# An LSTM recurrence on one core: partial sums placed ahead of an addition that waits, two more buffers, a shorter warm-up

## The chip, the cores and the metric

The kernel runs on one core of a Trainium2 chip. The metric is device time in microseconds of one execution, as the median of several runs. Below, TensorE is PE in the profile, VectorE is DVE, ScalarE is ACT, GpSimd is POOL, and SP is the queue of SyncE, which issues nearly all DMAs.

## The reference

An LSTM over 512 time steps with a batch of 32, 512 inputs and 512 hidden units, all in float32, whose hidden states are added to the input.

```python
xW = jnp.einsum('ntd,dg->ntg', x, Wx) + b          # 32 x 512 x 2048
def step(carry, xw_t):
    prev_h, prev_c = carry
    a = xw_t + prev_h @ Wh
    i, f, o = (jax.nn.sigmoid(a[:, k * Hd:(k + 1) * Hd]) for k in range(3))
    g = jnp.tanh(a[:, 3 * Hd:])
    next_c = f * prev_c + i * g
    next_h = o * jnp.tanh(next_c)
    return ((next_h, next_c), next_h)
out = x + hs                                        # hs: next_h of all steps
```

## The kernel before

Two kinds of work share the core. The first is the chain of time steps. Step k is `h_part(k)`, 32 products of the transposed h with Wh (line L667, 64 TensorE instructions), then `cell(k)`: three activations on ScalarE (L690 to L692), the cell's products and sum on VectorE (L693 to L695), a tanh (L696), h (L697) and its transposition (L702), which the next `h_part` waits for. GpSimd adds h to x for the output (L706) and, in `add_bias` (L648), the bias to the x product that `load_xw` (L645) has fetched for a later step; ScalarE copies that into PSUM as the seed of the gates (L654, L658).

The second is x times Wx, which fills TensorE behind each `h_part`. The first rows of eight time steps are done directly or in units (the head, until window `START` = 21, step 17). After that, rounds of 24 steps make three rows each: twenty products of sums of blocks of x with sums of blocks of Wx, each product again by seven smaller ones (line L412). A step k belongs to window v = k + 4, and its place in the round is (k - 17) mod 24, so that step 0 of a round opens it. Five of six windows start a new product (`begin`), and its seven parts are spread over windows v to v + 4 by `products`.

On the other engines a window's work is given out in a fixed order, and each engine works its own list in order:

- `evacuate(v)`: additions that are overdue; then `finish` of the second half of the product that began five windows ago and of the first half of that of four windows ago: half additions out of PSUM on VectorE (L559) or copies on ScalarE (L547); then ScalarE's copies of a newer product's accumulators (L440, L444), the addition L447 on VectorE, and for the product of three windows ago ScalarE's copies L451 and L452 into the PSUM tile `pp`, and VectorE's addition L453 into the same tile behind them.
- `run_due(v, room)`: from the list `due`, sorted by window, whatever is due, and then what fits in a room counted in columns (128 for a sum plus `FIXED` = 160, 512 for a node, 1024 for a whole addition). In it are sums of four blocks of x (L375 to L378, the x sums, which are a product's left factors), nodes (L347, sums of whole blocks of x), whole additions of products (L575), and in the head the sums of Wx's blocks (L246, L250).
- then `products(v)` for TensorE, `fetch(v)` for SyncE (factors of later products, rows of x), and `cell(k)`.

A half or whole addition takes its target from the list `free`, first in, first out: four tiles `slot`, and from `START` on four tiles that held blocks of Wx and their sums. A finished sum is stored to DRAM by four DMAs (`store`, L469) and its tile goes back to the list.

The head's x sums (`inner_sums`, L279 to L282) have four tiles of their own in the pool `spool`, one for each pair (row, half). Before the first products 24 matmuls on zeros are issued (L787).

Of the kernel before, what the change touches and what calls it, by code (L numbers as in the profile page):

```python
# [9 lines left out]
F32 = mybir.dt.float32  # L10
# [4 lines left out]
P = 128  # L15
B = 32
T = 512
NJ = 4
# [4 lines left out]
C = 256  # L23
# [21 lines left out]
NODES = 8  # L45
FIXED = 160
ROOM = 3400
HEAD_ROOM = 5000
SLACK = [1, 1, 3]
AHEAD = 3  # L50
# [54 lines left out]
def windows_of(k):  # L105

    return [k + 4]


START = windows_of(HEAD - LEAD)[0]  # L110
# [14 lines left out]
def kernel(  # L125
# [13 lines left out]
    spool = ctx.enter_context(tc.tile_pool(name="spool", bufs=4))  # L139
# [66 lines left out]
    def t_sums(i):  # L206
        w, t = raw[i], tt_[i]
        return [
            lambda: nc.vector.tensor_sub(t[:, 0:2], w[:, 1::2], w[:, 0:2]),
            lambda: nc.vector.tensor_sub(t[:, 2], w[:, 3], t[:, 0]),  # L210
            lambda: nc.vector.tensor_sub(t[:, 3], w[:, 2], t[:, 2]),
        ]

    def raw_factor(i, s):
        return raw[i][:, {1: 0, 2: 2, 3: 3}[s]] if s in (1, 2, 3) else tt_[i][:, {4: 3, 5: 0, 6: 2, 7: 1}[s]]
# [55 lines left out]

    def inner_sums(a, name):

        s = spool.tile([P, 4, 4, B], F32, name=f"s_{name}", tag="sums")
        v = nc.vector
        return [s[:, i] for i in range(4)], [
            lambda: v.tensor_add(s[:, 0], a(1, 0), a(1, 1)),  # L279
            lambda: v.tensor_sub(s[:, 1], s[:, 0], a(0, 0)),  # L280
            lambda: v.tensor_sub(s[:, 2], a(0, 0), a(1, 0)),
            lambda: v.tensor_sub(s[:, 3], a(0, 1), s[:, 1]),  # L282
        ]

    def block(src):

        return lambda g, e: src[:, 4 * g : 4 * g + 4, e]

    def raw_block(i, k):
        return rows[i][:, :, 2 * k : 2 * k + 2]  # L290
# [3 lines left out]
    due, order = [], count_from(0)  # L294
# [4 lines left out]
    def run_due(v, room):  # L299

        i = 0
        while i < len(due):
            window, _, columns, fn, ready = due[i]
            if window > v and (columns + FIXED > room or not ready(v)):
                i += 1
                continue
            assert ready(window)
            due.pop(i)
            fn()
            room -= columns + FIXED  # L310
            i = 0
# [68 lines left out]
    def left(a, s, sums):  # L380
        if s in (1, 2, 4):
            return a(*{1: (0, 0), 2: (0, 1), 4: (1, 1)}[s])
        return sums[{5: 0, 6: 1, 7: 2, 3: 3}[s]]
# [43 lines left out]
                if s == 4:  # L427
                    job.release()

    def evacuate(v):  # L430
        run_due(v - 0.5, 0)
        taken = 0
        for half, late in ((1, 5), (0, 4)):
            job = jobs.get(v - late)
            if job:
                taken += job.finish(half)
        job = jobs.get(v - 1)
        if job:
            job.pu = upool.tile([P, 2, C], F32, name=f"pu_{job.w}", tag="pu", bufs=4)
            nc.scalar.copy(job.pu[:, 0], job.acc)  # L440
        for job in (jobs.get(v - 1), jobs.get(v - 2)):
            if job and job.w5 == v - 1:
                job.p5 = upool.tile([P, C], F32, name=f"p5_{job.w}", tag="p5", bufs=4)
                nc.scalar.copy(job.p5, p5[:, 0])  # L444
        job = jobs.get(v - 2)
        if job:
            nc.vector.tensor_add(job.pu[:, 1], job.acc, job.p5)  # L447
            taken += C + FIXED
        job = jobs.get(v - 3)
        if job:  # L450
            nc.scalar.copy(job.pp[0], job.pu)  # L451
            nc.scalar.copy(job.pp[1][:, 0], job.acc)  # L452
            nc.vector.tensor_add(job.pp[1][:, 1], job.acc, job.p5)  # L453
            taken += C + FIXED
        return taken
# [3 lines left out]
    free = []  # L459
# [11 lines left out]
    def finish_unit(job, i, j):  # L471
        def finish(half):
            if half == 0:
                job.f = free.pop(0)
            nc.scalar.copy(job.f[:, half], job.pp[half].rearrange("p n c -> p (n c)"))
            if half:
                store(i, j, job.f)
                free.append(job.f)
            return 0

        return finish
# [37 lines left out]
    sums, left_uses = {}, {}  # L519
# [203 lines left out]
    head_sums = {}  # L723

    def prepare(v):

        job = jobs.get(v)
        ops = []
        if job is None or job.w >= START:
            return ops  # L730
        i, j = job.kind
        for k in range(2):
            if (i, k) not in head_sums:
                s, more = inner_sums(block(raw_block(i, k)), f"h{i}{k}")
                head_sums[i, k] = s
                ops += more
        job.factors = lambda s: [
            (left(block(raw_block(i, k)), s, head_sums[i, k]), raw_factor(NJ * k + j, s)) for k in range(2)
        ]
        job.finish = finish_unit(job, i, j)  # L740
        job.release = lambda: None
        return ops
# [3 lines left out]
    def announce(v):  # L746
        while later and later[0] <= v + AHEAD:
            job = jobs[later.pop(0)]
            describe(job, *job.kind)

    def describe(job, sb, n):
        if len(B_OF[n]) == 1:
            right = lambda s: raw_factor(B_OF[n][0][0], s)
        else:
            right = lambda s: job.ring[PLACE[s][0]][:, PLACE[s][1]]
        job.factors = lambda q: [(left(block(node(sb, A_OF[n])), q, job.sums), right(q))]
        job.finish = finish_product(job, sb, n)
        job.release = lambda: node_done(sb, A_OF[n])
        push_sums(job, sb, n)
# [23 lines left out]
    with tc.manual_schedule():  # L783
        warm = work.tile([P, G, P], F32, name="warm", tag="s")
        nc.scalar.activation(warm[:, 0], c_init, AF.Sigmoid)
        for m in range(6 * NJ):
            nc.tensor.matmul(  # L787
                pps[2][m % NJ * B : (m % NJ + 1) * B].rearrange("p n c -> p (n c)"),
                c_init[:, 0:B],
                c_init.unsqueeze(1).to_broadcast([P, 4, P]),  # L790
                start=True,
                stop=True,
            )
        nc.vector.transpose(
            bias_sb.rearrange("p (m l) -> p m l", l=B),
            bias_t.unsqueeze(2).to_broadcast([P, G * NJ, B]),
        )
        firsts = [gates[0], gates[1], pps[0], pps[1]]
        for q in range(4):
            for t in range(4):  # L800
                direct(t, firsts[t], (q,))
        for i in range(5):
            for op in t_sums(i):
                op()
        for op in prepare(0):
            op()
        products(0)
        for i in range(5, 8):
            for op in t_sums(i):
                op()  # L810
        push_factors()
        for t in range(4):
            keep_direct(t, firsts[t])
        for v, t in enumerate(range(4, ROW), 1):
            direct(t, gates[t % 2])
            for op in prepare(v):
                op()
            if v < 4:
                evacuate(v)
            run_due(0, 2400)  # L820
            keep_direct(t, gates[t % 2])
            if v < 4:
                products(v)
                fetch(v)
        seed_first(0)
        seed_last(0)
        seed_first(1)

        for k in range(T):
            if k % 2 == 0 and k + 2 < T:  # L830
                load_residual(k + 2)
            if 2 * 4 - 3 <= k and k + 3 < END:
                load_xw(k + 3)
            h_part(k)
            if 2 * 4 - 2 <= k and k + 2 < END:
                add_bias(k + 2)
            for m, v in enumerate(windows_of(k)):
                if v == START:
                    assert len(due) == 0 or due[0][0] >= START
                    free.extend(t.rearrange("p (h n) c -> p h (n c)", h=2) for t in others)  # L840
                announce(v)
                taken = evacuate(v)
                run_due(v, (ROOM if v >= START - 4 else HEAD_ROOM) - taken)
                products(v)
                tail_products(v)
                fetch(v)
                if k == T - 2:
                    x_last()
                if m == 0:
                    cell(k)  # L850
                    seed_first(k + 2)
                    seed_last(k + 1)
                for op in prepare(v + 1):
                    op()
        assert not due
# [51 lines left out]
```

## Time and profile before

| | |
|---|---|
| median of 3 runs | 3146.42 us (3145.94 to 3148.9) |
| profiled execution | 3145.59 us, span 3143.8 us |
| granted TensorE clock | 1.00 |
| busy: PE, DVE, ACT, POOL | 3121.6, 2177.2, 1604.4, 915.1 us |
| DMA queue q1, share of 16 engines | 61.6% |
| matmuls of L667 and L412 in the profile | 379 ns each, in groups that overlap |

Matmuls overlap and their ends are modelled, so PE's 99% doesn't say that it lost no time; how much it lost is read from the starts of the time steps in the timeline. Times of VectorE's instructions overlap a little too: the next one starts some 0.08 us before the end that is shown.

### The profile page before, as it was taken

Reading aid. Unit: us, or ns where it says so; the run is one execution under the profiler, and the core shown is the slowest. Engines: PE = TensorE matmul, PEld = TensorE weight load, DVE = VectorE, ACT = ScalarE, POOL = GpSimd, SP = SyncE. Lnnn points to the kernel's source line nnn. Section 1 sums busy time; section 2 is a strip of 40 time slices with the busy share of each in tenths; the row PEclk is TensorE's granted clock in tenths of the full one; section 3 lists DMA queues with packets and bytes.
Section 4 is the critical chain, followed back from the end, with each engine's and each line's share of the span. In section 5 each row is a group of like instructions: output and inputs, shape, how many; then the busy total and the mean of one; then the engine's idle time right before and its main releaser. Section 6 shows DMA issues by size and latency. Waiting matters only on the chain.

```text
span 3143.8 us, 133477 instructions
## 1 busy us (share of the span) xinstructions
PE 3121.6 (99%) x56656; PEld 1999.3 (64%) x56656; DVE 2177.2 (69%) x6107; ACT 1604.4 (51%) x4842; POOL 915.1 (29%) x1001
## 2 busy tenths in 40 slices
PE   9999999999999999999999999999999999999999
PEld 4666666666666666666666666666666666666544
DVE  5547777767676777777776767777777777676533
ACT  2455555555555555555555555555555555555433
POOL 0122323323232323233332323232333323232320
PEclk9999999999999999999999999999999999999999
DMA  6656675766675766757666757667576767575510
GB/s 225 218 160 211 209 226 185 233 201 222 206 230 178 228 204 209 235 180 232 201 221 208 237 173 234 198 213 231 180 231 197 225 203 231 183 240 190 162 60 25
DMA packets 316084, 631.63 MB, mean 201 GB/s; under 512 B 41952, under 2 KB 107744, under 8 KB 314976
## 3 DMA queue, kind: packets, MB, share of 16 engines
q1 hardware_dynamic: 315344, 623.09, 61.6%
q8 instruction: 446, 7.31, 1.0%
q14 instruction: 150, 1.23, 0.1%
q10 hardware_dynamic: 144, 0.01, 0.0%
HBM read 448.60 MB, written 174.33 MB: 198 GB/s over the span
## 4 chain that ended last, share of the span: by engine, by line
PE 89%; DVE 6%; DMA 2%; ACT 2%; issue 1%; SPq 1%; DVEq 0%; POOL 0%
PE gates L667 51%; PE pp L412 15%; PE acc L412 15%; PE p L412 5%; PE pp L600 1%; DMA xw<-xw 1%; DVE node L347 1%; PE acc L600 1%; ACT pp L451 1%; DMA xw<-slot 0%; DMA xw<-raw_sb 0%; ACT ig L696 0%; PE gates L600 0%; DVE c L695 0%; DVE fc L697 0%
## 5 line engine op out<-in xcount | busy, mean ns | idle before, releaser
L667 PE MATMUL gates<-wh_sb,ht 128*32 128x384 f32 x32704 | 1871.8, 379 | 15.5 <-DVE ht L702 14.6
L667 PEld LDWEIGHTS gates<-wh_sb,ht 128*32 128x32 f32 x32704 | 1120.0, 110 | 799.8 <-issue 670.5
L706 POOL TENSOR_TENSOR oc<-xr,ht 128x128 f32<-128x128 f32 x509 | 300.4, 590 | 2121.9 <-DVE ht L702 2102.1
L648 POOL TENSOR_TENSOR xw<-xw,bias_sb 128x512 f32<-128x512 f32 x488 | 631.6, 1294 | 88.8 <-DMA xw<-xw 42.3
L690 ACT ACTIVATE s<-gates 128x256 f32<-128x256 f32 x512 | 196.6, 384 | 797.0 <-PE gates L667 797.0
L453 DVE TENSOR_TENSOR pp<-acc,p 128x256 f32<-128x256 f32 x396 | 170.9, 432 | 248.3 <-ACT pp L452 234.5
L693 DVE TENSOR_TENSOR fc<-s,c 128x128 f32<-128x128 f32 x511 | 150.9, 295 | 239.1 <-ACT s L690 234.6
L697 DVE TENSOR_TENSOR fc<-s,ig 128x128 f32<-128x128 f32 x512 | 149.5, 292 | 192.7 <-ACT ig L696 192.7
L451 ACT COPY pp<-pu 128x512 f32<-128x512 f32 x396 | 237.3, 599 | 49.2 <-DVE slot L559 17.3
L412 PE MATMUL pp<-wb,node 128*32 128x256 f32 x3040 | 244.0, 379 | 0.0
L692 ACT ACTIVATE s<-gates 128x128 f32<-128x128 f32 x512 | 142.0, 277 | 188.5 <-PE gates L667 188.3
L654 ACT COPY gates<-xw 128x384 f32<-128x384 f32 x492 | 232.7, 473 | 4.9 <-DVE node L616 4.6
L696 ACT ACTIVATE ig<-c 128x128 f32<-128x128 f32 x512 | 158.7, 310 | 142.7 <-DVE c L695 117.0
L452 ACT COPY pp<-acc 128x256 f32<-128x256 f32 x396 | 142.3, 359 | 139.8 <-DVE slot L559 66.7
L702 DVE STREAM_TRANSPOSE ht<-fc 128x128 f32<-128x128 f32 x511 | 159.1, 311 | 55.5 <-DVE fc L697 2.7
L447 DVE TENSOR_TENSOR pu<-acc,p 128x256 f32<-128x256 f32 x396 | 162.3, 410 | 28.0 <-ACT p L444 27.7
L440 ACT COPY pu<-acc 128x256 f32<-128x256 f32 x396 | 147.2, 372 | 64.4 <-PE acc L412 64.4
L412 PE MATMUL acc<-wa,s 128*32 128x256 f32 x2128 | 171.0, 379 | 0.0
L412 PE MATMUL pp<-wb,s 128*32 128x256 f32 x2128 | 171.0, 379 | 0.0
L412 PE MATMUL acc<-wb,s 128*32 128x256 f32 x2128 | 170.5, 379 | 0.0
L412 PE MATMUL p<-wa,s 128*32 128x256 f32 x2128 | 170.4, 379 | 0.0
L695 DVE TENSOR_TENSOR c<-fc,ig 128x128 f32<-128x128 f32 x512 | 150.5, 294 | 17.7
(146 smaller groups left out, 4035.2 us busy)
## 6 DMA issues: line engine op xcount, KB each, us to landing
wb<-keep_b SPq DMA_DIRECT2D x266, 512.0 KB, 5.6
xw<-xw SPq DMA_DIRECT2D x488, 256.0 KB, 4.1
wa<-keep_a SPq DMA_DIRECT2D x266, 384.0 KB, 4.9
xw<-slot SPq DMA_DIRECT2D x624, 128.0 KB, 3.3
xr<-in_x_dram SPq DMA_DIRECT2D x256, 128.0 KB, 3.2
out_dram<-oc SPq DMA_DIRECT2D x255, 128.0 KB, 2.2
row<-in_x_dram SPq DMA_DIRECT2D x63, 512.0 KB, 6.8
xw<-raw_sb SPq DMA_DIRECT2D x252, 128.0 KB, 3.4
```

What stands on the lines that cost most here:

```text
L412: nc.tensor.matmul(dst[t * B : (t + 1) * B], a[:, t], w, start=s in (1, 5) and m == 0, stop=True, skip_group_check=True,)
L447: nc.vector.tensor_add(job.pu[:, 1], job.acc, job.p5)
L451: nc.scalar.copy(job.pp[0], job.pu)
L453: nc.vector.tensor_add(job.pp[1][:, 1], job.acc, job.p5)
L648: nc.gpsimd.tensor_add(xw[t], xw[t], bias_sb)
L654: nc.scalar.copy(gates[t % 2][:, 0:IFG], xw[t][:, 0:IFG])
L667: nc.tensor.matmul(g[j * B : (j + 1) * B, cols], state["ht"][:, k, :], wh_sb[:, k, j, cols], start=False, stop=True, skip_group_check=True,)
L690: nc.scalar.activation(s[:, 0:2], g[:, 0:2], AF.Sigmoid)
L693: nc.vector.tensor_mul(fc, s[:, 1], state["c"])
L696: nc.scalar.activation(tc_t, c, AF.Tanh)
L702: nc.vector.transpose(ht.rearrange("p q b -> p (q b)"), h)
L706: (nc.gpsimd if t < T - 3 else nc.vector).tensor_add(state["oc"][:, tt % 2], xr[t][:, tt % 2], ht)
```

## The change

- `evacuate` gets the window's room. At its front, `run_due` may now also take what is not yet overdue, up to 600 columns (`FIRST_SUMS`): two x sums, but no node.
- Between L447 and ScalarE's copies L451 and L452 a second `run_due` takes up to 1200 columns (`BETWEEN`) more, so that these stand on VectorE's list before L453. Both amounts are taken off the window's room, the second one whether used or not.
- The head's x sums are made in two tiles, each for both halves of a row, in place of four. When the rounds begin, two tiles of the same pool tag join `free`, which then has ten slots in place of eight.
- Twelve warming matmuls in place of 24.

In the built program the PE, ACT and POOL lists have the same operations in the same order, but for the twelve matmuls. VectorE's list has the same operations in another order; in SyncE's, two stores of a round stand one step later.

```diff
+FIRST_SUMS = 600
+BETWEEN = 1200
...
-    def inner_sums(a, name):
-        s = spool.tile([P, 4, 4, B], F32, name=f"s_{name}", tag="sums")
+    def inner_sums(a, s):
         v = nc.vector
-        return [s[:, i] for i in range(4)], [
+        return [s[:, g] for g in range(4)], [
...
-    def evacuate(v):
-        run_due(v - 0.5, 0)
-        taken = 0
+    def evacuate(v, room):
+        before = len(due)
+        run_due(v - 0.5, FIRST_SUMS)
+        taken = FIRST_SUMS if len(due) < before else 0
...
         job = jobs.get(v - 3)
         if job:
+            run_due(v, min(room - taken, BETWEEN))
+            taken += BETWEEN
             nc.scalar.copy(job.pp[0], job.pu)
             nc.scalar.copy(job.pp[1][:, 0], job.acc)
             nc.vector.tensor_add(job.pp[1][:, 1], job.acc, job.p5)
...
             if (i, k) not in head_sums:
-                s, more = inner_sums(block(raw_block(i, k)), f"h{i}{k}")
-                head_sums[i, k] = s
+                if (i, 0) not in head_sums:
+                    both = spool.tile([P, 2, 4, 4, B], F32, name=f"s_h{i}", tag="sums", bufs=2)
+                head_sums[i, k], more = inner_sums(block(raw_block(i, k)), both[:, k])
                 ops += more
...
-        for m in range(6 * NJ):
+        for m in range(3 * NJ):
...
             if v < 4:
-                evacuate(v)
+                evacuate(v, 0)
...
                     free.extend(t.rearrange("p (h n) c -> p h (n c)", h=2) for t in others)
+                    free.extend(spool.tile([P, 2, 2 * C], F32, name=f"slot_h{i}", tag="sums", bufs=2) for i in range(2))
                 announce(v)
-                taken = evacuate(v)
-                run_due(v, (ROOM if v >= START - 4 else HEAD_ROOM) - taken)
+                room = ROOM if v >= START - 4 else HEAD_ROOM
+                run_due(v, room - evacuate(v, room))
```

## The prediction

> **What bounds the kernel now.** I read the page's busy times and its groups first, then the chain of waits in order of time, and last the timeline of single steps.
>
> ```profile
> PE 3121.6 (99%) x56656; PEld 1999.3 (64%) x56656; DVE 2177.2 (69%) x6107; ACT 1604.4 (51%) x4842; POOL 915.1 (29%) x1001
> L667 PE MATMUL gates<-wh_sb,ht 128*32 128x384 f32 x32704 | 1871.8, 379 | 15.5 <-DVE ht L702 14.6
> L453 DVE TENSOR_TENSOR pp<-acc,p 128x256 f32<-128x256 f32 x396 | 170.9, 432 | 248.3 <-ACT pp L452 234.5
> ```
>
> ```profile
> 364.85 3.61 PE gates L667 x64
> 2819.81 3.66 PE gates L667 x64
> ```
>
> TensorE is never long idle, and VectorE sits 234.5 us in front of L453, which I call the waiting addition. That idle time costs nothing by itself: only TensorE's lost time counts, and 14.6 us of it is seen ahead of L667, waiting for the transposed h (L702). The last two rows are the same step of a round (24 steps), 17 rounds apart: 2454.96 / 17 = 144.41 us a round. Without a stall a step takes 6.04 us, or 5.61 us in the four steps of a round with five products in place of six (1213.60 to 1219.21 below is one), so a round would take 20 x 6.04 + 4 x 5.61 = 143.3. The loss is 1.1 us a round, 19.5 us in 18 rounds: the most that anything in the rounds can give back.
>
> Read step by step over those 408 steps it lies in four of the 24: the step that follows number 2 of the round starts late by 3.9 us in all rounds together, after number 3 by 4.5, number 4 by 7.3, number 13 by 2.8; the other twenty lose 0.9. Steps 3 and 4 of one round:
>
> ```profile
> 1213.60 3.66 PE L667 MATMUL gates<-wh_sb,ht 128*32 128x384 f32 x64
> 1218.45 0.31 DVE L702 STREAM_TRANSPOSE ht<-fc 128x128 f32<-128x128 f32 x1
> 1219.21 3.67 PE L667 MATMUL gates<-wh_sb,ht 128*32 128x384 f32 x64
> 1220.65 0.43 DVE L453 TENSOR_TENSOR pp<-acc,p 128x256 f32<-128x256 f32 x1 [0.98 <-ACT pp L452]
> 1222.48 1.28 POOL L648 TENSOR_TENSOR xw<-xw,bias_sb 128x512 f32<-128x512 f32 x1 [3.18 <-DMA xw<-slot]
> 1222.53 1.39 DVE L693 TENSOR_TENSOR fc<-s,c 128x128 f32<-128x128 f32 x1
> 1225.67 3.66 PE L667 MATMUL gates<-wh_sb,ht 128*32 128x384 f32 x64 [0.21 <-DVE ht L702]
> 1227.46 0.43 DVE L453 TENSOR_TENSOR pp<-acc,p 128x256 f32<-128x256 f32 x1 [1.63 <-ACT pp L452]
> 1227.81 0.28 DVE L375 TENSOR_TENSOR s<-row 128x128 f32<-128x128 f32 x1
> 1229.81 0.28 DVE L693 TENSOR_TENSOR fc<-s,c 128x128 f32<-128x128 f32 x1
> 1231.86 1.13 PE L667 MATMUL gates<-wh_sb,ht 128*32 128x384 f32 x9
> ```
>
> The last 1.13 is cut by the edge of the window asked for. Step 4 shows the mechanism: VectorE idles 1.63 us, does the waiting addition, and only then four x sums and two nodes (1227.81 to 1229.81, so 0.2 us a sum and 0.6 a node). The cell's first product (L693) starts 4.14 us into the step and the next step 6.19 after this one, 0.15 late. Step 2 shows the reserve: h is ready at 1218.76, 0.45 before TensorE wants it; in a 6.04 us step that is 0.88. So VectorE may reach L693 some 0.7 us late (0.3 in a short step) for nothing. Step 3 is another matter: the bias addition on GpSimd came late with its data, L693 took 1.39 instead of its mean of 0.29, and the next step came 0.42 late (6.46).
>
> **The change part by part.** *Sums ahead of the waiting addition* remove the mechanism of steps 4 and 13:
>
> ```profile
> 1279.77 3.66 PE L667 MATMUL gates<-wh_sb,ht 128*32 128x384 f32 x64
> 1281.98 0.43 DVE L453 TENSOR_TENSOR pp<-acc,p 128x256 f32<-128x256 f32 x1 [2.51 <-ACT pp L452]
> 1285.97 3.66 PE L667 MATMUL gates<-wh_sb,ht 128*32 128x384 f32 x64
> ```
>
> In step 13 (6.20, 0.16 late) five sums and a node follow the addition. In the changed order two sums stand at the head of the step, a node and a sum before the addition, and one sum behind it: it still starts some 2.2 us into the step, and L693 at about 3.3. All 2.8 go. In step 4 six sums are spread over the front and the idle 1.63 us, and two nodes go to step 7, where there is 0.88 of reserve: 7.1 of 7.3 go (0.2 kept for rounds in which the bias addition falls among the sums).
>
> *Two more slots.* Step 2 of the round before:
>
> ```profile
> 1068.42 3.64 PE L667 MATMUL gates<-wh_sb,ht 128*32 128x384 f32 x64
> 1071.40 0.69 DVE L559 TENSOR_TENSOR slot<-pp,slot 128x512 f32<-128x512 f32 x1 [1.97 <-PE gates L667]
> ```
>
> ```profile
> 1075.19 3.66 PE gates L667 x64
> ```
>
> L559's operands from TensorE were long done: it waited for its slot, whose last content was being stored by DMAs issued one step earlier. 6.77 instead of 5.61 us: 1.16 lost. With ten slots for eight the built order gives this addition a slot stored two steps earlier, and step 1's addition no store to wait for. All 3.9 go; nothing is added, since the slots take the memory of head tiles that are done by then.
>
> *What stays.* Step 3's late bias addition hangs on its load, not on sums; once step 2 no longer loses time, the data come later within step 3. Counted in the traced rounds, moved so, 8 of 18 fall on the cell at 3.3 to 3.7 us: 8 x 0.36 = 2.9 of 4.5 stay. The other twenty steps keep 0.9. Back so far: 3.9 + 1.6 + 7.1 + 2.8 = 15.4.
>
> *What is added: the waiting addition stands last.* Queued behind each added sum or node are L453 and, behind it, TensorE's first product of the step, which writes the same PSUM tile. It has no reserve:
>
> ```profile
> 1053.23 0.43 DVE L453 TENSOR_TENSOR pp<-acc,p 128x256 f32<-128x256 f32 x1
> 1053.72 0.64 PE L412 MATMUL acc<-wa,s 128*32 128x256 f32 x8
> ```
>
> The product starts 0.06 after the addition's end. It is wanted 3.45 us into a step. In most steps VectorE is through by 2.3 to 3.2. Step 22 is not such a step:
>
> ```profile
> 1189.43 3.67 PE L667 MATMUL gates<-wh_sb,ht 128*32 128x384 f32 x64
> 1190.42 0.36 ACT L452 COPY pp<-acc 128x256 f32<-128x256 f32 x1 [0.72 <-DVE slot L559]
> 1190.42 0.69 DVE L559 TENSOR_TENSOR slot<-raw_sb,slot 128x512 f32<-128x512 f32 x1
> 1190.83 1.42 POOL L648 TENSOR_TENSOR xw<-xw,bias_sb 128x512 f32<-128x512 f32 x1 [1.70 <-ACT pp L452]
> 1191.03 0.42 DVE L447 TENSOR_TENSOR pu<-acc,p 128x256 f32<-128x256 f32 x1
> 1191.36 0.42 DVE L453 TENSOR_TENSOR pp<-acc,p 128x256 f32<-128x256 f32 x1
> 1191.69 0.71 DVE L378 TENSOR_TENSOR s<-row,s 128x128 f32<-128x128 f32 x1
> 1192.88 0.64 PE L412 MATMUL acc<-t,s 128*32 128x256 f32 x8
> 2633.24 1.18 PE L667 MATMUL gates<-wh_sb,ht 128*32 128x384 f32 x12
> 2635.44 1.39 POOL L648 TENSOR_TENSOR xw<-xw,bias_sb 128x512 f32<-128x512 f32 x1 [1.81 <-DMA xw<-xw]
> ```
>
> Here the bias addition is late in all traced rounds but three (1.0 to 2.8 us into the step), and an operation with two SBUF inputs, like the sum L378, runs 0.71 instead of 0.29, ending 0.15 after the bias addition, while L447 and L453, with an input in PSUM, run through. Today L453 is past by then. In the new order a node and a sum stand before it. The node would start at 1191.37, finds GpSimd at work until 1192.25, and ends some 0.55 later, 1192.80 (the 0.15, and the 0.4 by which a node is longer); the sum ends 1193.00, L453 1193.35, and the product starts 1193.41 instead of 1192.88: 0.53. Where the bias addition comes later (2.20 in the other round shown) the node is through and the sum is held: L453 ends 4.26 into the step, 0.87. Where it comes earlier or after the sum, 0 to 0.6. The traced arrivals give 9.5 us in 18 rounds. [...]
>
> One move softens it. Of the whole additions (L575), two a round go from the end of step 11 or 17 to the front of the next one, and their stores of 512 KB with them. SyncE's queue takes them ahead of that step's fetches, which are for products one and two steps on. But the second store moves into a full stretch:
>
> ```profile
> 1159.00:1165.00 6.00, 6.00 (x116) 4.02 (x112) 4.50 (x11) 3.07 (x9) 1.67 (x3) 1.00 0.56 149
> 1165.00:1171.00 6.00, 6.00 (x119) 4.00 (x112) 4.65 (x14) 3.27 (x10) 1.66 (x3) 1.00 0.94 290
> ```
>
> At 290 GB/s it takes 1.8 us, so loads behind it land up to that much later, and part of step 22's bias additions move behind the sum (toll 5.0 at the full shift, 9.5 at none). I take 7.0.
>
> *Twelve warming matmuls fewer* I cost at nothing:
>
> ```profile
> 1.05 7.71 PE L787 MATMUL pp<-c_init 128*32 128x512 f32 x48 [1.05 <-DVE c_init L192]
> 18.14 0.29 DVE L279 TENSOR_TENSOR s_h<-row 128x128 f32<-128x128 f32 x1 [0.33 <-DMA row<-in_x_dram]
> 25.32 3.64 PE L600 MATMUL gates<-raw_sb,row 128*32 128x512 f32 x32 [1.10 <-DVE xw L616]
> ```
>
> TensorE could start its first real work up to 3.9 us sooner, but at 25.32 it waits for VectorE, whose queue has run without a gap since a DMA landed at 18.1: the gain turns into a longer wait there. Between 0 and +3.6 us (the 3.64 us behind that wait at half speed, if the array cools in it). [...]
>
> **The sum**: back 15.4, toll 7.0, small additions in steps 21 and 23 0.2: 8.2 us. The profiled execution took 3145.59 (span 3143.8), 0.83 below the median of 3146.42: 3137.4 against its own time, 3138.2 as a median.
>
> **Rivals.** [...]
>
> *No change.* If late loads, not late sums, set steps 3 and 4, the bias addition then falls on the cell there in every round, 0.41 each: 2 x 18 x 0.41 = 14.8, with the toll of 7.0 about the 19.5 of now, 3146 to 3150. Against it: in step 4 above the bias addition isn't near L693.
>
> *Slower.* The same toll in steps 21 and 23 too, because the store pushes their bias additions among the sums: 3 x 18 x 0.55 = 29.7 with 2.9 and 1.1 kept, against 19.5 now: +14.2, 3160.6. It decides where L453 ends later than 3.4 us into these steps; by the rows of step 23 it would end near 3.0.
>
> **How the numbers follow.** The forecast has 0.50 (3134 to 3142, by the toll's two ends and 0.8 us between runs), no toll 0.25, no change 0.15 (with a cooled array, +3.6), slower 0.10. A measurement of this kernel tells about 0.2% (6.3 us) from no change. Faster by more, below 3140.1: 0.25 and four fifths of 0.50, 0.65; within: 0.25; slower: 0.10. The range runs from 3129 to 3147.5.
>
> **What would show it.** Right: idle before L453 far below 234.5; step 4 and 13 at 6.04; step 2 at 5.61 with no held L559; in step 22 TensorE's first product released by the waiting addition, 0.3 to 0.9 late; a longer wait at 25 us and the clock unchanged. Wrong: h still late after steps 4 and 13, the product behind L453 late in many steps, or step 22 on time.

## The result, and the profile after

The changed kernel takes 3141.6 us (median of 22 runs, 3139.43 to 3143.83), the kernel before 3146.35 on the same chip (22 runs, 3143.17 to 3148.9): a ratio of 0.9984, 95% interval 0.9977 to 0.999. That is 4.75 us faster, where 8.2 were forecast. The profiled execution has a span of 3139.8 us against 3143.8, so 4.0 less.

First the page of the kernel after: the group of TensorE's h products, the group of the waiting addition (L457 now), and the chain of waits; the last row is the chain of the kernel before.

```profile
L671 PE MATMUL gates<-wh_sb,ht 128*32 128x384 f32 x32704 | 1861.1, 379 | 7.2 <-DVE ht L706 7.1
L457 DVE TENSOR_TENSOR pp<-acc,p 128x256 f32<-128x256 f32 x396 | 168.6, 426 | 63.1 <-ACT pp L456 63.1
PE gates L671 51%; PE pp L413 16%; PE acc L413 16%; PE p L413 5%; DMA xw<-xw 3%; PE pp L604 1%; DVE node L348 1%; DVE slot L563 1%; PE acc L604 1%; PE gates L604 0%; POOL xw L652 0%; DMA row<-in_x_dram 0%; DVE s L376 0%; PE p L604 0%; POOL oc L710 0%
```

```profile
PE gates L667 51%; PE pp L412 15%; PE acc L412 15%; PE p L412 5%; PE pp L600 1%; DMA xw<-xw 1%; DVE node L347 1%; PE acc L600 1%; ACT pp L451 1%; DMA xw<-slot 0%; DMA xw<-raw_sb 0%; ACT ig L696 0%; PE gates L600 0%; DVE c L695 0%; DVE fc L697 0%
```

TensorE's idle time ahead of its h products fell from 15.5 to 7.2 us, and VectorE's idle time ahead of the waiting addition from 248.3 to 63.1. But the chain has changed too: the load of the bias addition's data (DMA xw<-xw) went from 1% to 3%, and a half addition (DVE slot L563, 1%), the bias addition on GpSimd (POOL xw L652) and the first sum made from a node (DVE s L376), both shown as 0%, are new in it. A node (L347, now L348) stood there before. The gain is in the first two numbers, and the new names point to where something was paid for it.

The steps that lost time before, in the timeline of the kernel after; each row is the start of a step's h products:

```profile
1212.06 3.64 PE L671 MATMUL gates<-wh_sb,ht 128*32 128x384 f32 x64
1217.67 3.64 PE L671 MATMUL gates<-wh_sb,ht 128*32 128x384 f32 x64
1223.71 3.64 PE L671 MATMUL gates<-wh_sb,ht 128*32 128x384 f32 x64
1229.75 3.64 PE L671 MATMUL gates<-wh_sb,ht 128*32 128x384 f32 x64
...
1277.67 3.64 PE L671 MATMUL gates<-wh_sb,ht 128*32 128x384 f32 x64
1283.71 3.64 PE L671 MATMUL gates<-wh_sb,ht 128*32 128x384 f32 x64
```

The first four are steps 2, 3, 4 and 5 of a round, 5.61, 6.04 and 6.04 apart: nothing is lost. The last two are steps 13 and 14, 6.04 apart, where it was 6.20.

Step 22 pays. Two rounds, in the order of start; the columns are start, duration, engine, line, operation, out<-in:

```profile
466.87 3.66 PE L671 MATMUL gates<-wh_sb,ht 128*32 128x384 f32 x64
468.21 1.49 POOL L652 TENSOR_TENSOR xw<-xw,bias_sb 128x512 f32<-128x512 f32 x1 [1.67 <-DMA xw<-xw]
468.81 1.44 DVE L348 TENSOR_TENSOR node<-row,node 128x512 f32<-128x512 f32 x1
470.28 0.29 DVE L376 TENSOR_TENSOR s<-node 128x128 f32<-128x128 f32 x1
470.49 0.42 DVE L457 TENSOR_TENSOR pp<-acc,p 128x256 f32<-128x256 f32 x1
470.97 0.64 PE L413 MATMUL acc<-t,s 128*32 128x256 f32 x8 [0.43 <-DVE pp L457]
473.59 3.64 PE L671 MATMUL gates<-wh_sb,ht 128*32 128x384 f32 x64
...
610.97 3.64 PE L671 MATMUL gates<-wh_sb,ht 128*32 128x384 f32 x64
612.92 1.77 POOL L652 TENSOR_TENSOR xw<-xw,bias_sb 128x512 f32<-128x512 f32 x1 [2.31 <-DMA xw<-xw]
613.60 1.25 DVE L376 TENSOR_TENSOR s<-node 128x128 f32<-128x128 f32 x1
615.24 0.64 PE L413 MATMUL acc<-t,s 128*32 128x256 f32 x8 [0.64 <-DVE pp L457]
```

In the first the bias addition starts 1.34 into the step, and the node, 0.68 elsewhere, takes 1.44. The waiting addition ends 4.04 into the step, the product starts 4.10 in, and the next step comes 6.72 after this one: 0.68 late. In the second the bias addition comes at 1.95; the node is through, the sum is held (1.25 for 0.29), and the product starts 4.27 into the step.

Added up over rounds 2 to 18 (17 of them, from the starts of all steps in each trace, less 6.04 or 5.61 a step; a dash is under 0.1 us), with the experiments that follow:

| kernel | median us | ratio to before, 95% interval | first step at | lost in step 2 | 3 | 4 | 13 | 22 | 23 | all 24 |
|---|---|---|---|---|---|---|---|---|---|---|
| before | 3146.35 | 1 | 60.47 | 3.87 | 4.28 | 6.96 | 2.67 | - | 0.64 | 18.5 |
| after | 3141.60 | 0.9984 (0.9977 to 0.999) | 62.10 | - | 0.45 | - | - | 12.81 | - | 13.3 |
| e1: 24 warming matmuls | 3139.63 | 0.9982 (0.9974 to 0.9991) | 60.34 | - | 0.62 | - | - | 12.94 | - | 13.5 |
| e2: step 22 freed | 3132.90 | 0.9960 (0.9948 to 0.9973) | 62.15 | - | 0.53 | - | - | 0.95 | 3.71 | 5.4 |
| e3: no bias addition in step 22 | 3126.44 | 0.9944 (0.9931 to 0.9956) | 60.64 | - | 1.04 | - | - | - | - | 0.9 |
| e4: e2, warming in the wait | 3134.28 | 0.9968 (0.9955 to 0.998) | 60.36 | - | 1.10 | - | - | 0.51 | 3.83 | 5.4 |
| e5: slots alone | 3142.90 | 0.9995 (0.9986 to 1.0004) | 60.57 | - | 5.18 | 6.89 | 2.79 | - | 0.31 | 15.6 |
| e6: order alone | 3141.30 | 0.9990 (0.9981 to 0.9999) | 60.44 | 0.19 | 0.87 | - | - | 12.99 | - | 14.0 |
| e7: steps 22 and 23 freed | 3138.99 | 0.9981 (0.9972 to 0.999) | 60.51 | - | - | - | - | 1.14 | 7.89 | 9.1 |
| e8: node of step 22 made in 21 | 3128.57 | 0.9949 (0.9937 to 0.9962) | 60.73 | - | 0.18 | - | - | 0.27 | 1.03 | 1.4 |
| e9: before, 12 warming matmuls | 3146.32 | 1.0007 (0.9998 to 1.0015) | 62.33 | 1.86 | 3.23 | 9.53 | 2.67 | - | 1.09 | 18.6 |
| e10: e8 with eight slots | 3129.86 | 0.9955 (0.9941 to 0.9968) | 60.45 | 0.63 | 1.39 | - | - | 0.36 | 1.24 | 3.8 |

The groups e1 to e4, e5 to e8 and e9 to e10 ran on three different chips, so medians are compared through the ratio, each to the kernel before on its own chip. The times lost are those of one profiled execution each. How far a single step of one execution can be trusted is seen in e9, whose rounds run the code of the kernel before: steps 2, 3 and 4 lose 1.86, 3.23 and 9.53 us there in place of 3.87, 4.28 and 6.96, with nearly the same sum. Differences of that size in one step are not put down to an edit below.

The span's 4.0 us, all 18 rounds: 18.7 saved outside step 22, 13.5 paid in it, 1.6 paid before the first step, 0.5 saved between the first step and the first round, 0.1 paid in the tail. -18.7 + 13.5 + 1.6 - 0.5 + 0.1 = -4.0.

### The profile page after: what moved, and what is told of

It is laid out like the page before. It is cut to its first block, busy times and chain, and to the rows that moved or that the text cites. A ratio compares the mean times of both kernels' runs of the same rounds, so it can differ in the third digit from the quotient of the medians.

```text
span 3139.8 us, 133260 instructions
## 1 busy us (share of the span) xinstructions
PE 3113.1 (99%) x56632; PEld 1797.3 (57%) x56632; DVE 2248.2 (72%) x6107; ACT 1615.8 (51%) x4842; POOL 983.1 (31%) x1001
## 4 chain that ended last, share of the span: by engine, by line
PE 90%; DMA 4%; DVE 3%; issue 2%; SPq 1%; POOL 1%; ACT 0%; POOLq 0%; DVEq 0%
PE gates L671 51%; PE pp L413 16%; PE acc L413 16%; PE p L413 5%; DMA xw<-xw 3%; PE pp L604 1%; DVE node L348 1%; DVE slot L563 1%; PE acc L604 1%; PE gates L604 0%; POOL xw L652 0%; DMA row<-in_x_dram 0%; DVE s L376 0%; PE p L604 0%; POOL oc L710 0%
## 5 line engine op out<-in xcount | busy, mean ns | idle before, releaser
L671 PEld LDWEIGHTS gates<-wh_sb,ht 128*32 128x32 f32 x32704 | 1022.3, 110 | 877.9 <-issue 755.4
L710 POOL TENSOR_TENSOR oc<-xr,ht 128x128 f32<-128x128 f32 x509 | 357.2, 702 | 2010.6 <-DVE ht L706 1996.6
L652 POOL TENSOR_TENSOR xw<-xw,bias_sb 128x512 f32<-128x512 f32 x488 | 640.8, 1313 | 128.0 <-DMA xw<-xw 71.9
L697 DVE TENSOR_TENSOR fc<-s,c 128x128 f32<-128x128 f32 x511 | 154.1, 302 | 376.4 <-ACT s L694 374.8
L413 PE MATMUL pp<-wb,node 128*32 128x256 f32 x3040 | 235.0, 379 | 0.0
L457 DVE TENSOR_TENSOR pp<-acc,p 128x256 f32<-128x256 f32 x396 | 168.6, 426 | 63.1 <-ACT pp L456 63.1
L413 PE MATMUL acc<-wa,s 128*32 128x256 f32 x2128 | 164.6, 379 | 0.0
L413 PE MATMUL pp<-wb,s 128*32 128x256 f32 x2128 | 164.5, 379 | 0.0
L446 ACT COPY p<-p 128x256 f32<-128x256 f32 x396 | 149.6, 378 | 28.2 <-PE p L413 20.6
```

The costliest lines, as they stand in the source:

```text
L413: nc.tensor.matmul(dst[t * B : (t + 1) * B], a[:, t], w, start=s in (1, 5) and m == 0, stop=True, skip_group_check=True,)
L652: nc.gpsimd.tensor_add(xw[t], xw[t], bias_sb)
L671: nc.tensor.matmul(g[j * B : (j + 1) * B, cols], state["ht"][:, k, :], wh_sb[:, k, j, cols], start=False, stop=True, skip_group_check=True,)
L697: nc.vector.tensor_mul(fc, s[:, 1], state["c"])
L710: (nc.gpsimd if t < T - 3 else nc.vector).tensor_add(state["oc"][:, tt % 2], xr[t][:, tt % 2], ht)
```

## Experiments: what step 22 and the start cost

The theory: the saving is whole, and is eaten by step 22, where GpSimd's bias addition, running at the same time, holds a node or a sum ahead of the waiting addition (1.44 us for 0.68, 1.25 for 0.29 above), and by TensorE's clock, which in the kernel after falls to 0.50 behind a wait at the start. The main rivals: the toll comes from the order by itself; the start is late for another reason.

**e1**, the warming alone undone.

```diff
-        for m in range(3 * NJ):
+        for m in range(6 * NJ):
```

> The changed kernel with 24 warming matmuls in place of 12; nothing else differs. Theory (the array cools while TensorE waits 2.74 us at 22.5 us, and the 32 matmuls behind the wait then take 5.34 us for 3.64): the wait shrinks below 1.2 us, the 32 matmuls take 3.6 again, the first step starts at 60.5 us in place of 62.1, and the time is 1.6 us under the changed kernel, about 3140.0, that is 6.4 under the kernel before. Rival (the late first step comes from the order of VectorE's work in the head, not from TensorE): the first step stays at 62.1 and the time at 3141.6.

The same matmuls behind the wait at 25 us, in the timelines of the kernel after, of e1 and of e3 (which has 12 warming matmuls too); then the clock in windows (the third number from the end) of after and of e3.

```profile
25.25 5.34 PE L604 MATMUL gates<-raw_sb,row 128*32 128x512 f32 x32 [2.74 <-DVE xw L620]
```

```profile
25.18 3.64 PE L604 MATMUL gates<-raw_sb,row 128*32 128x512 f32 x32 [1.17 <-DVE xw L620]
```

```profile
25.49 3.64 PE L604 MATMUL gates<-raw_sb,row 128*32 128x512 f32 x32 [2.93 <-DVE xw L620]
```

```profile
26.00:29.00 3.00, 3.00 (x20) 0.79 (x16) 3.00 (x6) 0.00 (x0) 0.00 (x0) 0.50 0.63 240
```

```profile
26.00:29.00 3.00, 3.00 (x36) 0.91 (x32) 3.00 (x7) 0.00 (x0) 0.00 (x0) 1.00 0.64 241
```

As the theory had it: with 24 the wait is 1.17, the clock stays whole (1.00 from 26 to 29 us) and the first step starts at 60.34. But the price is not there in every execution. e3 waited longer than the changed kernel (2.93 against 2.74), kept its clock (1.00) and started at 60.64. In the kernel after the clock fell to 0.50 at about 26.0 and came back at about 29.4. So the length of the wait alone doesn't tell whether the clock falls; what else does is not shown. In the ratios (0.9984 and 0.9982) the difference doesn't show. It does within the 22 runs of the kernel after: 16 had a mean clock of 0.999 and a median of 3141.8, six had 1.0 and 3140.1; of e1's 11 runs three had 0.999. Only the profiled executions show where the clock fell.

**e2**, step 22 freed. The second `run_due` is left out in step 22 of a round, nothing else.

```diff
+            if v < START or (v - START) % PER != 22:
-            run_due(v, min(room - taken, BETWEEN))
+                run_due(v, min(room - taken, BETWEEN))
```

> The changed kernel, but in step 22 of each round (there alone) no node and no sum stands before the waiting addition. Theory (all of the toll, 14.5 us in 19 rounds, is TensorE's first product of step 22 behind a held waiting addition): step 22 takes 6.04 in all rounds, the other steps stay as they are, and the time falls by 14 us to 3127.6, 18.8 under the kernel before. Rival (the work that is held goes elsewhere: the node and sum behind the addition hold the cell of step 22 or the products of step 23): 3 to 8 us come back in steps 22 and 23, 3131 to 3136.

Step 22's toll goes, 12.81 to 0.95 us, but step 23 loses 3.71. The rival was right in kind and in price: 4.7 us are lost in the two steps, and 3132.9 lies in its range. So taking the node out of the way of the waiting addition isn't enough; why is seen in e7 and e8.

**e3**, the order kept and the collision taken away: the bias addition of step 22 is not done.

```diff
-            if 2 * 4 - 2 <= k and k + 2 < END:
+            if 2 * 4 - 2 <= k and k + 2 < END and (k + 4 < START or (k + 4 - START) % PER != 22):
                 add_bias(k + 2)
```

> The changed kernel with its order kept whole, but GpSimd's bias addition of step 22 of each round is left out (so the bias is missing from one time step in 24; nothing else is left out). [...] Rival (the toll is the order by itself, four SBUF operations ahead of the waiting addition being too many): a part of the toll of at least 0.3 us a round stays, 3133 or more.

Step 22 of e3, node, sum, waiting addition and product in the same order as in the kernel after:

```profile
1181.58 3.66 PE L671 MATMUL gates<-wh_sb,ht 128*32 128x384 f32 x64
1183.52 0.68 DVE L348 TENSOR_TENSOR node<-row,node 128x512 f32<-128x512 f32 x1
1184.23 0.29 DVE L376 TENSOR_TENSOR s<-node 128x128 f32<-128x128 f32 x1
1184.44 0.42 DVE L457 TENSOR_TENSOR pp<-acc,p 128x256 f32<-128x256 f32 x1
1185.04 0.64 PE L413 MATMUL acc<-t,s 128*32 128x256 f32 x8
```

The node takes 0.68 and the sum 0.29, the waiting addition ends 3.28 into the step, the product starts at 3.46 and waits for nothing. The 17 rounds together lose 0.9 us. The toll is the collision and not the order: 19 GpSimd instructions of 1.3 us fewer, and the kernel is at 0.9944 of before.

**e4**, e2 with twelve more warming matmuls where TensorE waits at 22.5 us.

```diff
         products(0)
+        for m in range(3 * NJ):
+            nc.tensor.matmul(
...
```

> Step 22 without node and sum before the waiting addition, and 12 more warming matmuls, which stand behind the first products, where TensorE waits for VectorE at 22.5 us. Theory: step 22 at 6.04 (14 us less) and, since the array does not cool, the 32 matmuls behind the wait at 3.64 and the first step at 60.5 (1.6 less): 3126.0, 20.4 under the kernel before. Rival for the start (12 warming matmuls fewer at the very beginning are what is missing, wherever others stand): first step at 62.1 or, if the fill delays TensorE, later, 3127.6 or more.

In the profiled execution, at 3130.4, the wait is 0.24 us, the 32 matmuls take 3.64 and the first step starts at 60.36, as expected. The median, 3134.28, is not below e2's: the other five runs took 3134.0 to 3136.7 and had a mean clock of 0.999 in place of 1.0. They left no trace, so where their clock fell is open; e8 shows below that there is a second place.

## Experiments: the parts alone, and the chain behind step 22

**e5**, the slots alone: the changed kernel with `FIRST_SUMS = 0`, no second `run_due`, and 24 warming matmuls.

```diff
-FIRST_SUMS = 600
+FIRST_SUMS = 0
...
-            run_due(v, min(room - taken, BETWEEN))
-            taken += BETWEEN
```

> The kernel before with the two more slots alone (VectorE's order around the waiting addition as before, 24 warming matmuls). Theory (each part does its own piece): step 2 gives back its 3.9 us and step 3 the 1.6 that the prediction gave it, steps 4 and 13 keep their 7.3 and 2.8, step 22 has no toll: 3.9 to 5.5 us less than before, 3141 to 3142.5. Rival (step 3's late bias addition follows from step 2's stall, so it goes wholly with the slots): 8 us less, about 3138. Rival (the slots do nothing without the new order): 3146.

Step 2's 3.87 goes, but steps 3, 4 and 13 keep their losses (5.18 in step 3, where the order of the kernel before lost 4.28 and, in e9, 3.23). The ratio, 0.9995, can't be told from 1: the theory's gain of 3.9 to 5.5 us isn't shown, and the rival that the slots alone do nothing can't be ruled out; the traced rounds lose 2.9 us less. Step 3 of one round of e5, 6.45 long:

```profile
928.90 3.66 PE L669 MATMUL gates<-wh_sb,ht 128*32 128x384 f32 x64
930.35 0.43 DVE L455 TENSOR_TENSOR pp<-acc,p 128x256 f32<-128x256 f32 x1 [0.97 <-ACT pp L454]
930.69 0.68 DVE L348 TENSOR_TENSOR node<-node,row 128x512 f32<-128x512 f32 x1
932.02 0.28 DVE L377 TENSOR_TENSOR s<-s,node 128x128 f32<-128x128 f32 x1
932.18 1.47 POOL L650 TENSOR_TENSOR xw<-xw,bias_sb 128x512 f32<-128x512 f32 x1 [3.18 <-ACT s L692]
935.36 0.85 PE L669 MATMUL gates<-wh_sb,ht 128*32 128x384 f32 x8 [0.20 <-DVE ht L704]
```

The node and four sums stand behind the waiting addition and end at 3.40; the bias addition begins at 3.28, on the cell. In the changed order two of these sums are made ahead of a half addition for which VectorE would wait anyway, so that the cell isn't met, or only by its last part.

**e6**, the order alone: no slots added, 24 warming matmuls.

```diff
-                    free.extend(spool.tile([P, 2, 2 * C], F32, name=f"slot_h{i}", tag="sums", bufs=2) for i in range(2))
```

> The changed kernel without the two more slots and with 24 warming matmuls: VectorE's new order alone. Theory: steps 4 and 13 run at 6.04 (10.1 us back), step 2 keeps its wait for the store (3.9), step 22 pays its toll of 13 to 14.5: about as much slower as step 22 costs beyond 10.1, 3149 to 3151, slower than the kernel before. Rival (the new order alone makes all the gain and the slots are idle): 3139.6, as the changed kernel with 24.

The theory missed and the rival was nearer: 0.999, faster and not slower. Step 2 loses 0.19 us where the theory left it 3.9. Its half addition is still held for its slot, but less: it starts 1.38 us into the step on average and 2.23 at the latest, where it was 1.81 and 2.98 before. And three sums stand behind it, not four. That one sum of 0.2 us fewer, at the times at which the half addition started before, would have left 2.3 us of loss, so the larger part is that the slots came free earlier; why they did is open. The two parts overlap: each alone clears step 2 or nearly so, and with the new order there the slots bring 0.5 us in the rounds (14.0 against e1's 13.5), which is too little to be told from the spread between executions.

**e7**, no node and no sum ahead of the waiting addition in steps 22 and 23 (`not in (22, 23)` in the place of e2's condition), 24 warming matmuls; and **e8**, the same with 1200 columns more room in step 21, so that step 22's node and sum are made there, behind its waiting addition.

```diff
-                run_due(v, room - evacuate(v, room))
+                run_due(v, room + (1200 if v >= START and (v - START) % PER == 21 else 0) - evacuate(v, room))
```

> The changed kernel with 24 warming matmuls, and no sum and no node ahead of the waiting addition in steps 22 and 23 (only the last two steps of a round differ). With step 22 alone freed, step 23 lost 4.2 us in 18 rounds: its bias addition starts 0.1 to 0.5 into the step, a half addition is held until it ends, and the waiting addition, with one sum before it, ends at 3.42 to 3.82 where 3.39 is wanted. Theory (that sum of 0.20 is what is too much): step 23 keeps 0 to 0.22 a round, 1.2 us in all, step 22 its 1.1: 3139.6 - 13.7 + 2.3, 3128. Rival (what is held in step 23 is the half additions, and taking the sum away only moves the wait): step 23 keeps 4 us, 3131.

> As e7, and the node and sum that stand in step 22 are made in step 21, behind its waiting addition (1200 columns more room there); step 22 then has no node and no sum at all. Theory (all that is left in step 22 is the node that the bias addition holds ahead of the cell): step 22 loses nothing, step 21 nothing since its VectorE work ends about 3.5 us into the step, step 23 up to 1.2 in all: 3126 to 3127. Rival (step 21's bias addition now holds the node there instead): step 21 loses 0.2 to 0.5 a round, 3130 to 3135.

e7 lost more in step 23 than e2, 7.89 us: the rival, and at twice its price. The turn from step 22 to 23 in the same round, first of e7, then of e8:

```profile
755.29 1.53 POOL L653 TENSOR_TENSOR xw<-xw,bias_sb 128x512 f32<-128x512 f32 x1 [2.88 <-DMA xw<-xw]
755.71 1.25 DVE L376 TENSOR_TENSOR s<-node 128x128 f32<-128x128 f32 x1
758.86 0.62 POOL L711 TENSOR_TENSOR oc<-xr,ht 128x128 f32<-128x128 f32 x1 [2.04 <-DVE ht L707]
758.93 3.66 PE L672 MATMUL gates<-wh_sb,ht 128*32 128x384 f32 x64
759.44 1.28 POOL L653 TENSOR_TENSOR xw<-xw,bias_sb 128x512 f32<-128x512 f32 x1
759.79 1.48 DVE L564 TENSOR_TENSOR slot<-raw_sb,slot 128x512 f32<-128x512 f32 x1
762.63 0.28 DVE L377 TENSOR_TENSOR s<-s,node 128x128 f32<-128x128 f32 x1
763.06 0.64 PE L413 MATMUL acc<-wa,s 128*32 128x256 f32 x8 [0.47 <-ACT s L697]
```

```profile
756.62 0.62 POOL L711 TENSOR_TENSOR oc<-xr,ht 128x128 f32<-128x128 f32 x1 [2.06 <-DVE ht L707]
757.20 1.28 POOL L653 TENSOR_TENSOR xw<-xw,bias_sb 128x512 f32<-128x512 f32 x1
757.43 3.64 PE L672 MATMUL gates<-wh_sb,ht 128*32 128x384 f32 x64
757.55 1.48 DVE L564 TENSOR_TENSOR slot<-raw_sb,slot 128x512 f32<-128x512 f32 x1
760.40 0.28 DVE L377 TENSOR_TENSOR s<-s,node 128x128 f32<-128x128 f32 x1
760.89 0.61 PE L413 MATMUL acc<-wa,s 128*32 128x256 f32 x8
```

It is one collision that makes the next. In e7 step 22's bias addition holds the sum in front of the cell (1.25 for 0.29), so h comes late; GpSimd's output addition (L711) waits for h, and behind it on GpSimd stands step 23's bias addition, whose data are there. It starts 0.51 into step 23 and holds the half addition (1.48 for 0.69) until 2.34 into the step. The waiting addition then ends at 3.79, the sum L377 behind it at 3.98, and TensorE's first product, which takes that sum, starts at 4.13: 0.68 after the 3.45 at which it is wanted, and 0.68 is what the step loses. (The profile puts this wait down to ScalarE's L697. But in 11 of e7's 19 rounds that instruction ends only after the product's start, and in all 18 late ones the product starts 0.15 after the sum's end.) So the sum has to be done for this product wherever it stands. In e2 it stood before the waiting addition, and a late round lost at most 0.44; behind it, it comes later still, which is why e7 loses more. In e8 no node and no sum stands in step 22 to be held. The output addition starts 0.81 before step 23 and the bias addition 0.23 before it; the half addition takes the same 1.48 but ends 1.60 into the step, the sum ends at 3.25 and the product starts at 3.46, in time. In the kernel after, the toll hid this second collision: with step 22 late by 0.38 to 0.98, step 23's bias addition was done in time. e8's rounds lose 1.4 us, near the theory's 1.2. The time falls short of it (3126 to 3127 would be a ratio of about 0.9937), and 0.9949 is still the lowest ratio of the versions that leave nothing out, though the intervals of e2 and e10 overlap with its own.

e8's trace holds one late step more, in the tail. Two rows of its timeline, one of its windows:

```profile
2934.64 1.38 POOL L653 TENSOR_TENSOR xw<-xw,bias_sb 128x512 f32<-128x512 f32 x1 [2.91 <-ACT s L695]
2934.81 1.35 DVE L699 TENSOR_TENSOR ig<-s 128x128 f32<-128x128 f32 x1
2937.72 5.35 PE L672 MATMUL gates<-wh_sb,ht 128*32 128x384 f32 x64 [2.72 <-DVE ht L707]
```

```profile
2938.00:2941.00 3.00, 3.00 (x24) 1.34 (x20) 0.00 (x0) 0.00 (x0) 1.33 (x2) 0.50 0.23 81
```

Where the products of x have run out, a bias addition fell on the cell (1.35 for 0.28), TensorE's wait grew to 2.72 from the 1.65 of the kernel after, and the clock fell to 0.50: h products of 3.66 took 5.35. Together that is 2.8 us. e10's profile has it too, with a wait of 2.50, a clock of 0.50 and h products of 5.26.

**e9**, the kernel before with 12 warming matmuls, and **e10**, e8 without the two slots; both diffs are as in e1 (the other way) and e6.

> The kernel before with 12 warming matmuls in place of 24, nothing else. [...] Rival (the shorter warm-up brings the first work forward, and the gain is kept): 1 to 3 us under the kernel before.

> As e8, but without the two more slots (eight, as in the kernel before). Theory (the new order alone takes step 2's loss from 3.9 to 0.2 us, since three sums stand behind the held half addition there and not four): 0.3 to 1 us above e8 in the profile, so about the same ratio to the kernel before, 0.995. Rival (with steps 22 and 23 on time the stores of steps 0 and 1 and the loads crowd and step 2's wait grows again): 3 to 4 us above e8, ratio 0.996.

In e9's profiled execution the clock fell (0.52 on average from 26 to 29 us, 5.28 for the 32 matmuls behind a wait of 2.97) and its first step starts at 62.33, 1.9 later; the median, at 1.0007 with an interval that holds 1, can't be told from no change, but the rival's gain of 1 to 3 us is ruled out. e10 loses 2.4 us more in the rounds than e8, 0.63 of it in step 2 and 1.2 in step 3: more than the 0.3 to 1 of the theory, less than the rival's 3 to 4. That is one execution of each; the intervals of the ratios, 0.9955 and 0.9949, overlap, so what the slots are worth on top of the new order is not settled.

## Why the prediction came out as it did

The result lies in the range, and the mechanism named for the gain and for the toll is the one the runs show. Three terms were off, and they partly cancel: 3.3 us too little was given to the saving, 6.5 too little to the toll and 1.6 too little to the warming. That the time came within 3.4 us of the 3138.2 forecast is in part luck, and it lies just above 3140.1, in the part to which the prediction gave 0.25 and not in that to which it gave 0.65. (Its losses by step, 4.5, 7.3 and 2.8, are those of 18 rounds and not of the 408 steps it names, which are 17.)

- *Steps 4 and 13.* Right: 6.96 and 2.67 us all went, as the table shows, and e5 shows that the order and not the slots did it.
- *Step 2.* The size was right (3.87). The cause given, the slots, is one of two that would each do (e5 and e6).
- *Step 3.* The step that failed is the sentence that its late bias addition "hangs on its load, not on sums", with 2.9 us kept. The order took the loss to 0.45; with the slots alone it stayed (5.18). The load is late either way: the bias addition starts 0.68 to 3.58 into the step before and 1.05 to 4.52 after. But what it met were the sums and the cell behind them, and these moved. Before, the cell started 3.26 to 4.41 into step 3; after, at 3.25 in all 17 rounds. The bias addition still falls on the cell's first product in eight of them (0.64 to 1.21 for 0.29), but with nothing late ahead of it the step's reserve takes all or most of that. With steps 21 and 23 and the first round the saving was 18.7, not 15.4.
- *Step 22.* Right place and mechanism, which e3 shows; the mis-sized term is the toll, 7.0 forecast, 13.5 measured. A single hit was priced nearly right: 0.53 against 0.65 measured, 0.87 against 0.85. The count was wrong. Early and late bias additions had been given little or nothing, and some were to move behind the sum through the moved store. In the 17 rounds every one started 0.32 to 2.33 into the step and every round paid, 0.38 to 0.98. None came behind the sum, and two early ones (0.85 and 0.87 into the step) cost 0.91 and 0.93, since they held the half addition ahead of the node (1.70 and 1.73 for 0.69).
- *The warming.* Taken at nothing, it cost 1.6 us in the profiled execution, within the stated bounds of 0 to 3.6. That the clock would fall in the longer wait was the case noted there, and the sign "the clock unchanged" did not come (0.50 behind 2.74 us); e3 shows that the clock may as well stay at 1.00 (behind 2.93). No run shows the 3.6: it was the author's estimate, for which all 32 matmuls behind the wait would run at half the clock. They took 5.34 for 3.64 in the kernel after and 5.28 in e9, so 1.6 to 1.7 us more.
- *Rivals.* No toll, with the 15.4 kept whole and a time of 3131, is what e3 makes true by leaving out the bias addition. No change needed the bias addition on the cell in steps 3 and 4 in every round, and they lose 0.45 and nothing. The slower rival needed tolls in steps 21 and 23, and these lose nothing here; e2 and e7 show that step 23 can, once step 22 is on time.

What the prediction read off the sum L378 held for the node: it took 1.44 beside a bias addition (the kernel after, at 468.81), 0.68 without one (e3).

## What to carry to other kernels

Work put in front of an instruction that another engine waits for needs its price at the worst neighbour it can meet, in every round, not at its duration alone: here 0.97 us of node and sum became up to 2.1. When a collision costs time, look at whether moving the held instruction or the holder ends the chain, for the first repair (e2) passed 3.7 us on to the next step, and only emptying the step (e8) kept the gain. And when two parts of a change aim at one stall, try each alone, since their gains need not add.

## What the runs showed of the hardware

- GpSimd was held as well as VectorE. In the timeline of the kernel after, an output addition (L710), which took 0.46 at 1217.29 (0.61 is the median of 509), took 1.35 beside a whole addition; the bias addition of 1.28 took 1.77 beside a node and a sum in the second round of step 22 above.

```profile
1199.00 1.18 DVE L579 TENSOR_TENSOR slot_h<-raw_sb 128x1024 f32<-128x1024 f32 x1
1199.16 1.35 POOL L710 TENSOR_TENSOR oc<-xr,ht 128x128 f32<-128x128 f32 x1 [4.17 <-DVE ht L706]
1217.29 0.46 POOL L710 TENSOR_TENSOR oc<-xr,ht 128x128 f32<-128x128 f32 x1 [3.44 <-DVE ht L706]
```

- How long TensorE waited did not by itself tell whether its clock fell. Behind waits of 2.74 us in the kernel after and 2.52 in e2 at the start, and of 2.72 in e8 and 2.50 in e10 in the tail, the granted clock was 0.50; behind 2.97 in e9 it was 0.52 on average from 26 to 29 us. Behind 2.93 in e3 it stayed at 1.00, as it did behind 1.10 in the kernel before, 1.17 in e1, and 1.65 in the tail of the kernel after. What else decided it is not shown.
